# Four preactivated convolution layers, layer 3: a widest state for each query row, far key tiles scored at strips only and packed into banks, and two places a step for other products

## The chip, the cores and the metric

One core of one Trainium2 chip runs the whole kernel as one program. The metric is the device time of that program in microseconds, as the median of several runs. A profiled execution has a time of its own, which stands beside the others in the table below.

## The reference, cut to what matters

The input is an image batch `x` of 4 x 256 x 48 x 48 in float32. Each of four layers adds its own result to `x`, after a group norm `_gn`. Layers 0 to 2 are convolutions. Layer 3 is a box-window linear attention with 8 heads of 32 channels:

```python
q = sigmoid(einsum('bchw,oc->bohw', x, Wq)); k = sigmoid(einsum(..., Wk))
v = einsum(..., Wv); v = v / max(norm(v, axis=1), 1e-12)
Ik  = integral(k)
Ikv = integral(einsum('bfhw,bghw->bfghw', k, v))
for w in (1, 2, 4):                     # window of 48 / w rows and columns around each pixel
    wk, wkv = box(Ik, 48 // w), box(Ikv, 48 // w)
    attn = einsum('bdhw,bdfhw->bfhw', q, wkv)
    norm = einsum('bdhw,bdhw->bhw', q, wk)
    outs.append(attn / (norm[:, None] + 1e-06))
return einsum('bchw,oc->bohw', concatenate(outs, axis=1), Wout) + bout
```

For each pixel and each of three windows the result is the sum over the pixels in the window of (q . k) v, divided by the sum of (q . k). The windows reach 24, 12 and 6 pixels to one side, less one on the other (`HALVES`). There is no softmax, so a sum over keys that all queries of a set see may be taken as a state, the sum of k v^T, which q then multiplies.

## The kernel before, in words

Layers 0 to 2 take the span up to about 1412 us, layer 3 the rest. Near the end of layer 2 some of layer 3's projections are already made.

**Tiles of layer 3.** The 48 rows are six tile rows of `RB` = 8. A query block is one tile row of 8 x 48 = 384 queries (`NB`), of one image `b` and one half of the channels `ct` (four heads, `HG`). `order` runs over 4 images x 2 halves x 6 rows, 48 blocks. A key tile is 8 rows x 16 columns = 128 keys; a tile row `a` has three (`NKC`), index `c`. A block goes over all key tile rows that its widest window sees (`tiles_of`), at most three away, in two halves of the width (`PARTS`): that is one step, 60 for the six blocks of a half of the channels, 480 in all. Near tile rows (the smallest window sees them, at most one away) and far ones take turns.

**A step.** `Block.scores` multiplies keys by queries on TensorE into two PSUM tiles `s` of two banks each, two heads a tile, up to 512 columns a head; the four heads stand on four row strips of the array. A penalty product of bf16 (`picks`, `masks`) adds -1024 where the widest window does not see the key. `Block.masked` takes them out into `sm`: ACT (and, for tiles three rows away, DVE for one of the two pairs) applies a Relu for the widest window; DVE multiplies the middle window's part by a mask; POOL multiplies a part of that by the smallest window's mask. Two steps later (`LAG`) `Block.sums` multiplies `sm` by the values `vs` into three accumulators `acc0` to `acc2`, on four column strips of the array.

**The state.** For tile rows at most two away (`rows_whole`), a query column of the widest window sees whole key tiles except at strips (`strips`): 8 or 16 of the columns of a key tile. Only the strips are summed in steps; for the rest `state` makes k v^T of each tile row (keys transposed on TensorE, `keys_ps`; then `kv_ps`), `window_state` adds the rows that a query block sees on POOL into `kv`, and `Block.whole` multiplies it by the queries, one product for each head and key column, of 24 or 32 query columns by 8 rows (192 or 256 columns, three for each head). Tiles three rows away are in no state: they are scored and summed at all their columns, `rows_seen` giving 7 or 8 query rows.

**Other products.** Projections of the next image, key states, norms, output products and divisions are generators in `active`; `advance()` moves each by one `yield` and is called once a step, after the sums. The estimates `spare` (TensorE) and `slack` (POOL) say whether a job may go on in this step (`turn`, `bank`, `pool_turn`); all share the one PSUM bank `st` of `ps_m`. `until(...)` calls `advance()` until something is made, with no limit on cost. `FETCH` is the number of calls between a load's issue and its use. Every engine runs its instructions in the program's order, and SP issues nearly all loads and stores in one queue.

**Norms.** `k_sums` makes box sums of the keys (POOL, DVE's scans, ACT; stored to `kb_d` by way of `pt`); `norms` loads upper and lower rows (`nhi`, `nlo`) and the queries (`nq`), subtracts and multiplies on POOL, and sums on TensorE (`norm_ps`). `inverse`, `prepare` and `finish` divide, multiply by `Wout` (`out_ps`) and store. A block cannot begin before the block two before it is done, and that needs its norm.

All of layer 3's instructions carry line 244 in the profile, since a helper records them; they are told apart by the names of tiles.

Of the kernel before, what the change touches and what calls it, by code (L numbers as in the profile page):

```python
# [22 lines left out]
P = 128  # L23
# [4 lines left out]
RB = 8  # L28
# [56 lines left out]
MIDWAY, WHOLE = 3, 4  # L85
# [55 lines left out]


# [3 lines left out]
def penalties():  # L146

    got = []
    for half in range(2):
        got.append(((0, half), strips(half), None))  # L150
    for da, (r0, r1) in FAR_ROWS.items():
        for half in range(2):
            got.append(((da, half), PARTS[half], (r0, r1)))
    return got
# [22 lines left out]
def window_masks():  # L177
# [15 lines left out]
    for key, parts, rows in penalties():  # L193
        at = PENALTY_AT[key][0]
        for c, x0, x1 in parts:
            xs = np.arange(x0, x1)[None, :, None]
            ys = np.arange(*(rows or (0, RB)))[None, None, :]
            n = (x1 - x0) * ys.size
            kx = c * KC + np.arange(KC)[:, None, None]
            ky = key[0] * RB + np.arange(RB)[:, None, None]  # L200
            unseen = ~((xs - h <= kx) & (kx < xs + h)) & (ys == ys)
            costs[RB : RB + KC, at : at + n] = UNSEEN * unseen.reshape(KC, n)
            if rows is not None:
                unseen = ~((ys - h <= ky) & (ky < ys + h)) & (xs == xs)
                costs[0:RB, at : at + n] = UNSEEN * unseen.reshape(RB, n)
            at += n
    ms += [np.tile(m, (P // D, 1)) for m in (picks, costs)]
    return np.concatenate(ms + [column_taps()], axis=1).astype(np.float32)
# [39 lines left out]
def conv_preact_kernel(  # L248
# [75 lines left out]
    kf_d = [dram.tile([C, HW], F32, tag=f"kf{b}", name=f"kf_d{b}") for b in range(B)]  # L324
    kb_d = [dram.tile([NW, C, H, W], F32, tag=f"kb{b}", name=f"kb_d{b}") for b in range(B)]
# [14 lines left out]
    def advance(time=ALL, pool_time=ALL):  # L340
# [3 lines left out]
        spare = min(spare, 0.0) + time  # L344
        slack = min(slack, 0.0) + pool_time
# [57 lines left out]
    free = {"xr": 1, "xn": 2, "kt": 2, "sq": 2, "vt": 2, "cs": 1, "o": 2, "rc": 2, "res": 2}  # L403

    FETCH = 3
# [187 lines left out]
    with (  # L593
# [107 lines left out]
        def load_constants():  # L701
            sync.dma_start(out=w2_sb, in_=w2)
            sync.dma_start(out=b1_sb, in_=b1.rearrange("(p o) -> p o", o=1))
            sync.dma_start(out=taps, in_=masks_in[:QB, NMASK:])
# [918 lines left out]
    with (  # L1623
# [25 lines left out]
        nc.gpsimd.memset(zeros, 0.0)  # L1649
        head_sel = wts.tile([P, NCT, D], F32, name="head_sel")  # L1650
# [12 lines left out]
        inside = wts.tile([P, (RB + 1) * ROW], F32, name="inside")  # L1663
        nc.gpsimd.memset(inside, 1.0)
        for r in range(RB + 1):
            nc.gpsimd.memset(inside[:, r * ROW + GAP - 1 : r * ROW + GAP], 0.0)
# [10 lines left out]
        def k_sums(mo):  # L1677
# [14 lines left out]
            for at, (b, a) in enumerate(todo):  # L1692
# [27 lines left out]
                for i, j in ((0, n // 2), (n // 2, n)):  # L1720
                    dve.tensor_tensor_scan(
                        cs[:, i:j],
                        inside[:, i:j],
# [5 lines left out]
                    yield 1  # L1729
# [3 lines left out]
                pt = scr.tile([P, NW, RB, W], F32, tag="pt", name="pt")  # L1733
                for wi, h in enumerate(HALVES):
# [5 lines left out]
                    yield 1  # L1740
# [6 lines left out]
                )  # L1747
                made.add(("kb", b, mo, a))

        def norms(b, rb):  # L1750
# [4 lines left out]
            def load(ct):  # L1755
                chans = slice(ct * P, (ct + 1) * P)
                hi = scr.tile([P, NW, RB, W], F32, tag="nhi", name="nhi")
                lo = scr.tile([P, NW, RB, W], F32, tag="nlo", name="nlo")
                qf = scr.tile([P, NB], F32, tag="nq", name="nq")
                sync.dma_start(out=qf, in_=qr_d[b][chans, rb * NB : (rb + 1) * NB])  # L1760
                for wi, h in enumerate(HALVES):
# [7 lines left out]
                    if n < RB:  # L1769
# [3 lines left out]
                        )  # L1773

                    y0 = rb * RB - h - 1
# [5 lines left out]
                return hi, lo, qf  # L1781
# [5 lines left out]
            loaded = [load(ct) for ct in range(NCT)]  # L1787
            yield FETCH
            for hi, lo, qf in loaded:
# [9 lines left out]
                sums.append(hi)  # L1799
            yield 1  # L1800
# [49 lines left out]
        def state(b, ct, a):  # L1850
# [3 lines left out]
            yield FETCH  # L1854
            yield from bank(1, product_time(NKC * P))
# [15 lines left out]
            act.copy(states[b, ct][:, a], ps)  # L1871
            made.add(("state", b, ct, a))

        def window_state(i):
# [4 lines left out]
            yield from wait_for(*(("state", b, ct, a) for a in rows))  # L1879
            st = states[b, ct]  # L1880
            yield from pool_turn(NKC * D, len(rows) - 1, urgent=True)
            t = scr.tile([P, NKC, D], F32, tag="kv", name="kv", bufs=2)
            pool.tensor_add(t, st[:, rows[0]], st[:, rows[1]])
            for a in rows[2:]:
                pool.tensor_add(t, t, st[:, a])
            wides[i] = t
            made.add(("window", i))

        def load_q(b, ct, rb):
# [5 lines left out]
            return qs  # L1895
# [12 lines left out]

        class Block:


            def __init__(self, i, qs):
                self.i, self.qs = i, qs
                self.b, self.ct, self.rb = b, ct, rb = order[i]
                self.tiles = tiles_of(rb)
                self.todo = [
                    [(a, half) for a, half in self.tiles if seen(wi, a, rb)] for wi in range(NW)
                ]
                self.accs = self.stage = None

            def scores(self, a, half):
                r0, r1 = rows_seen(0, a, self.rb)
                ss = [ps_s.tile([P, 2, 512], F32, tag="s", name="s") for _ in range(NPR)]
                at = 0
                for c, x0, x1 in PARTS[half]:
                    n = (x1 - x0) * (r1 - r0)
                    for pr, s in enumerate(ss):
                        for j in range(2):
# [4 lines left out]
                                self.qs[head, x0:x1, r0:r1],  # L1933
                                start=(at == 0),
                                stop=False,
                            )
                    at += n
                lo, hi = strip_columns(half) if rows_whole(a, self.rb) else (0, at)
                first, n = PENALTY_AT[(0 if rows_whole(a, self.rb) else a - self.rb), half]
                for pr, s in enumerate(ss):  # L1940
                    for j in range(2):
                        g = 2 * pr + j
                        rows = slice(g * D, g * D + RB + KC)
                        pe.matmul(
                            s[:, j, lo:hi],
                            picks[rows, :],
                            masks[rows, PEN_AT + first : PEN_AT + first + n],
                            start=False,
                            stop=True,
                        )  # L1950
                return ss

            def parts(self, wi, a, half):

                if wi == 0:
                    return strips(half) if rows_whole(a, self.rb) else PARTS[half]
                return parts_seen(wi, half)

            def masked(self, a, half, ss):

                rb = self.rb
                r0, r1 = rows_seen(0, a, rb)
                wis = [wi for wi in range(NW) if seen(wi, a, rb)]
                full = rows_whole(a, rb)
                offset = {PARTS[half][0][0]: 0}
                offset[PARTS[half][1][0]] = (PARTS[half][0][2] - PARTS[half][0][1]) * (r1 - r0)
                left = {c: x0 for c, x0, _ in PARTS[half]}

                t = smp.tile([P, NPR * SM_ROOM], F32, tag="sm", name="sm")
                at, blocks_, views = 0, [], {}  # L1970
                for wi in wis:
                    y0, y1 = rows_seen(wi, a, rb)
                    ps = self.parts(wi, a, half)
                    for c, p0, p1 in ps:
                        if wi == 0:
                            continue
                        n = HG * (y1 - y0) * (p1 - p0)
                        views[wi, c] = t[:, at : at + n].rearrange(
                            "p (j x r) -> p j x r", j=HG, r=y1 - y0
                        )  # L1980
                        at += n
                    if wi > 0:
                        continue
                    n = sum(p1 - p0 for _, p0, p1 in ps) * (y1 - y0)
                    block = t[:, at : at + HG * n].rearrange("p (j n) -> p j n", j=HG)
                    blocks_ = [block[:, 2 * pr : 2 * pr + 2] for pr in range(NPR)]
                    at, o = at + HG * n, 0
                    for c, p0, p1 in ps:
                        m = (p1 - p0) * (y1 - y0)
                        views[wi, c] = block[:, :, o : o + m].rearrange(  # L1990
                            "p j (x r) -> p j x r", r=y1 - y0
                        )
                        o += m
                assert at <= NPR * SM_ROOM

                def times_mask(engine, wi, c, rows, cols, dst, src):
                    mr = rb * RB + rows[0] - (a * RB - HALVES[wi] + 1)
                    mc = cols[0] - (c * KC - MCOL0[wi])
                    nr, ncol = rows[1] - rows[0], cols[1] - cols[0]
# [5 lines left out]
                many = seen(NW - 1, a, rb)  # L2005

                def middle(s, pr):
                    y0, y1 = rows_seen(1, a, rb)
                    for c, p0, p1 in parts_seen(1, half):
                        at = offset[c] + (p0 - left[c]) * RB  # L2010
                        src = s[:, :, at : at + (p1 - p0) * RB].rearrange(
                            "p j (x r) -> p j x r", r=RB
                        )[:, :, :, y0:y1]
                        dst = views[1, c][:, 2 * pr : 2 * pr + 2]
                        times_mask(dve, 1, c, (y0, y1), (p0, p1), dst, src)

# [365 lines left out]
```

## Time and profile before

| | us |
|---|---|
| median of 3 runs | 3204.7 |
| lowest and highest run | 3195.62, 3205.02 |
| the profiled execution | 3220.09 |
| its span, first to last instruction | 3218.3 |
| first score product of layer 3, from the span's start | 1412.0 |

| busy in the span | us | share |
|---|---|---|
| TensorE matmul (PE) | 2886.4 | 90% |
| TensorE weight load (PEld, overlaps PE) | 2014.6 | 63% |
| VectorE (DVE) | 2004.0 | 62% |
| GpSimd (POOL) | 1351.2 | 42% |
| ScalarE (ACT) | 1018.9 | 32% |

The mean granted clock of TensorE is 0.952 of full speed. How to read the lines shown later: a group is a line, engine, operation, tiles written and read, shape and count, then busy us, mean ns of one, then the engine's idle time before them and what ended it. For TensorE, 32\*128 is the part of the array in use, rows by columns. An f32 matmul leaves two records. A timeline line is start, duration, engine, operation and count. A wait line is who waited for whom, us in total, times, and the longest.

### The profile page before, as it was taken

To read this page: it belongs to the slowest core of one execution; us is meant where nothing else is said; L and a number is where in the kernel's file an instruction comes from. 1 tells how busy PE (TensorE), PEld (TensorE's weight loads), DVE (VectorE), ACT (ScalarE), POOL (GpSimd) and SP (SyncE) were. 2 spreads that over 40 slices of the span, in tenths; PEclk is the share of its full clock that TensorE was granted. 3 is DMA by queue.
4 is the path that set the end of the run, shared out by engine and by line. 5 is a ranking of instruction groups with operands and counts; after the bars stand their busy time and mean duration, and the time that the engine had idled before them with its cause. 6 is when DMAs were issued, how large, how long until landed. Compare 5 with 4: busy or idle time off the path is not lost.

```text
span 3218.3 us, 97296 instructions
## 1 busy us (share of the span) xinstructions
PE 2886.4 (90%) x41802; PEld 2014.6 (63%) x41802; DVE 2004.0 (62%) x3907; ACT 1018.9 (32%) x2090; POOL 1351.2 (42%) x1916
## 2 busy tenths in 40 slices
PE   3678999899989978889996999998999999999999
PEld 2456768678776857576663665565566665666665
DVE  7976668647855731466774765676546775455454
ACT  0002211111111153326642335552336533333322
POOL 0000021003001221146788776877846777634443
PEclk9789899999999997989998999999999999999999
DMA  8746513431342253224466555554734455501222
GB/s 273 213 158 196 162 53 116 130 107 60 125 132 92 74 152 114 103 89 140 157 207 173 172 167 164 167 171 152 193 91 145 141 173 162 160 33 54 86 68 67
DMA packets 380033, 433.85 MB, mean 135 GB/s; under 512 B 129844, under 2 KB 335444, under 8 KB 378452
## 3 DMA queue, kind: packets, MB, share of 16 engines
q1 hardware_dynamic: 378403, 425.76, 42.9%
q8 instruction: 331, 5.42, 0.7%
q0 software_dynamic: 144, 1.08, 0.2%
q10 hardware_dynamic: 1056, 0.79, 0.1%
q14 instruction: 99, 0.80, 0.1%
HBM read 287.91 MB, written 140.68 MB: 133 GB/s over the span
## 4 chain that ended last, share of the span: by engine, by line
PE 60%; DVE 12%; POOL 4%; DMA 4%; ACT 4%; issue 3%; SPq 2%; ACTq 0%; DVEq 0%; POOLq 0%
PE s L244 16%; PE cv L244 15%; PE acc L244 14%; PE out_ps L244 5%; PE proj_ps L244 5%; DVE sm L244 3%; PE ap L244 2%; ACT sm L244 2%; SPq L244 2%; DVE l2v L244 2%; POOL nhi L244 1%; POOL sm L244 1%; DVE v L244 1%; PE keys_ps L244 1%; DVE x L244 1%
## 5 line engine op out<-in xcount | busy, mean ns | idle before, releaser
L244 DVE TENSOR_TENSOR sm<-s,masks 128x448 f32<-128x448 f32 (+11 forms) x1536 | 634.6, 470 | 465.5 <-PE s L244 431.5
L244 POOL TENSOR_TENSOR sm<-sm,masks 128x704 f32<-128x704 f32 (+11 forms) x512 | 595.2, 1184 | 559.1 <-DVE sm L244 558.7
L244 ACT ACTIVATE sm<-s 128x384 f32<-128x384 f32 (+2 forms) x864 | 467.5, 545 | 783.1 <-PE s L244 641.0
L244 PE MATMUL s<-qs,ks 32*128 32x320 f32 (+3 forms) x7680 | 601.6, 402 | 46.7 <-ACT sm L244 41.6
L244 PE MATMUL cv<-vx,wt 128*128 128x288 f32 x2080 | 561.6, 426 | 91.1 <-DVE vx L244 49.6
L244 PE MATMUL acc<-sm,vs 128*32 128x128 f32 (+20 forms) x17920 | 607.4, 279 | 1.4 <-issue 1.4
L244 PEld LDWEIGHTS s<-qs,ks 32*128 32x128 f32 x7680 | 376.9, 186 | 278.1 <-issue 111.0
L244 PEld LDWEIGHTS acc<-sm,vs 128*32 128x32 f32 x17920 | 430.2, 110 | 190.5 <-issue 137.6
L244 PEld LDWEIGHTS cv<-vx,wt 128*128 128x128 f32 x2080 | 403.4, 198 | 213.0 <-issue 54.1
L244 POOL MEMSET v<- 128x16 f32 (+1 forms) x120 | 18.7, 216 | 761.1 <-DVE vx L244 634.3
L244 PE MATMUL cv<-v,wl 128*128 128x384 f32 x1152 | 227.9, 358 | 25.1 <-issue 8.0
L244 PEld LDWEIGHTS cv<-v,wl 128*128 128x128 f32 x1152 | 217.7, 198 | 36.6 <-issue 16.4
L244 DVE TENSOR_SCALAR sm<-s 128x896 f32<-128x896 f32 (+1 forms) x96 | 110.9, 1155 | 144.4 <-PE s L244 125.4
L244 PE MATMUL s<-masks 24*128 24x192 bf16 (+2 forms) x1920 | 175.5, 268 | 0.0
L244 POOL TENSOR_TENSOR v<-l2v,v 128x384 fp32r<-128x384 f32 x96 | 108.5, 1160 | 119.3 <-ACT v L244 110.6
L244 PE MATMUL cv<-pad,wl 128*128 128x384 bf16 x864 | 145.5, 331 | 5.1 <-ACT pad L244 5.1
L244 POOL TENSOR_TENSOR nhi<-nhi,nq 128x384 f32<-128x384 f32 x144 | 147.8, 1048 | 0.0
L244 PEld LDWEIGHTS <-wl 128*128 128x128 bf16 x864 | 84.5, 98 | 65.6 <-issue 8.1
L244 PE MATMUL out_ps<-o,wout_sb 128*32 128x384 f32 x1152 | 119.8, 487 | 4.9 <-DVE res L244 2.2
L244 DVE TENSOR_TENSOR pt<-cs 128x184 f32<-128x184 f32 x144 | 119.8, 836 | 0.1
L244 PE MATMUL out_ps<-stage,wout_sb 128*32 128x384 f32 x1152 | 119.4, 486 | 0.0
L244 PE MATMUL ap<-seen,xT 120*128 120x120 f32 (+3 forms) x832 | 118.8, 302 | 0.0
(178 smaller groups left out, 3434.7 us busy)
## 6 DMA issues: line engine op xcount, KB each, us to landing
wt<-wt SPq DMA_DIRECT2D x48, 768.0 KB
kb_d<-pt SPq DMA_DIRECT2D x48, 576.0 KB
rc<-r_d SPq DMA_DIRECT2D x192, 144.0 KB
nhi<-kb_d SPq DMA_DIRECT2D x120, 192.0 KB
nlo<-kb_d SPq DMA_DIRECT2D x88, 192.0 KB
o_d<-stage SPq DMA_DIRECT2D x24, 576.0 KB
o<-o_d SPq DMA_DIRECT2D x24, 576.0 KB
wl<-wl_d SPq DMA_DIRECT2D x16, 768.0 KB
```

The source lines that it names most:

```text
L244: return lambda *args, **kwargs: self.tc.keep_in_program_order(op(*args, **kwargs))
```

## The change

- Tile rows two or three away get one step for their strips of all three key columns (384 columns, or 336 where 7 rows are seen) instead of two steps of 512 or 448. The middle window's pieces of tile rows two away are scored apart, each put into the first far step whose bank has room; where none has, a step without strips is added. Tile rows at most one away stay as they were. A half of the channels has 50 steps instead of 60.
- So that tiles three away need strips alone, the state now depends on the query's row: `window_state` makes `wide`, eight states, one for each query row. Seven of them hold a part of the far tile row's keys: the values are multiplied by 0 or 1 per key (`row_parts`, 21 ACT copies), multiplied by the transposed keys (`part_ps`, 12 products of 224 columns), and added to the base on DVE. The transposed keys are stored by `state` to `kt_d` and loaded again. `Block.whole` makes a product for each key column, query row and head, of 24 or 32 columns; it reads the queries in another order, `qr`, which is loaded beside `qs`.
- All widest Relus are on ACT.
- `advance()` is called twice a step: before the sums with the step's estimate, and after them with none. The whole state is added at step 2 of a block and not 4 (`WHOLE`); `window_state` of the next block starts when a block begins and not midway; `FETCH` is 5 calls and not 3. In the first pass the key tile rows are loaded one block earlier.
- `norms` loads the lower rows and the queries of one half of the channels at a time, from single buffers, the second after the first half's POOL work. `pt` has one buffer. DVE's two scans are cut at a row.

```diff
-MIDWAY, WHOLE = 3, 4
+MIDWAY, WHOLE = 3, 2
...
-    FETCH = 3
+    FETCH = 5
...
+        if time is not None:
+            spare = min(spare, 0.0) + time
+            slack = min(slack, 0.0) + pool_time
...
+            lo, qf = load_lower(0)
             yield FETCH
-            for hi, lo, qf in loaded:
+            for ct, hi in enumerate(loaded):
...
+                if ct + 1 < NCT:
+                    lo, qf = load_lower(ct + 1)
+                    yield FETCH
...
             act.copy(states[b, ct][:, a], ps)
+            sync.dma_start(out=kt_d[b][ct, a], in_=kt.rearrange("p c n -> p (c n)"))
...
+            keys = scr.tile([P, NKC, P], F32, tag="keys1", name="keys1", bufs=1)
+            sync.dma_start(out=keys.rearrange("p c n -> p (c n)"), in_=kt_d[b][ct, far])
+            yield from pool_turn(NKC * D, len(rows), urgent=True)
+            base = scr.tile([P, NKC, D], F32, tag="kv", name="kv", bufs=2)
+            wide = scr.tile([P, NKC, RB, D], F32, tag="wide", name="wide", bufs=2)
...
+            if above:
+                pool.tensor_copy(wide[:, :, 0], base)
+            else:
+                pool.tensor_add(wide[:, :, 0], base, st[:, far])
...
+                part = scr.tile([P, HG, RB - 1, D], F32, tag="part", name="part", bufs=1)
+                for y in range(RB - 1):
+                    at = y if above else RB - 1 + y
+                    act.activation(
+                        part[:, :, y], vs, AF.Identity, scale=row_parts[:, at : at + 1]
+                    )
+                    if y % 3 == 2:
+                        yield 1
...
+                    pe.matmul(
+                        ps[head, at : at + n],
+                        keys[:, c, head],
+                        part[:, g].rearrange("p y d -> p (y d)"),
...
+                dve.tensor_add(
+                    wide[:, c0 : c + 1, 1:],
...
+            for n, a, c in sorted(middles, key=lambda m: -m[0]):
+                fits = [st for st in far if st.columns + n <= 512]
+                if not fits:
+                    far.append(Step(rb))
...
-                if full:
-                    widest(act, *second)
-                    middle(*first)
-                    widest(act, *first)
-                    middle(*second)
-                else:
-                    widest(act, *first)
-                    widest(dve, *second)
+                widest(*second)
+                middle(*first)
+                widest(*first)
+                middle(*second)
...
-                            t[head, c, :],
-                            self.qs[head, c0:c1],
...
+                                self.accs[0][head].rearrange("p (w r) -> p w r", w=W)[:, c0:c1, y],
+                                t[head, c, y, :],
+                                self.qr[head, y, c0:c1],
...
+            advance(max(time, 500.0), max(pool_time, 150.0))
             if n >= LAG:
...
-            advance(max(time, 500.0), max(pool_time, 150.0))
+            advance(None)
```

## The prediction, made before the changed kernel ran

> **What bounds the kernel now.** I read the page's busy times first, then the windows of layer 3, then its groups by shape, then TensorE's timeline, then the waits. A measurement of this kernel can tell about 0.3%, 10 us, from no change.
>
> ```profile
> span 3218.3 us, 97296 instructions
> ...
> PE 2886.4 (90%) x41802; PEld 2014.6 (63%) x41802; DVE 2004.0 (62%) x3907; ACT 1018.9 (32%) x2090; POOL 1351.2 (42%) x1916
> ```
>
> ```profile
> core 0: us, PE busy (x) PEld busy (x) DVE busy (x) ACT busy (x) POOL busy (x), PEclk, DMA share, GB/s
> 1412.00:3218.00 1806.00, 1701.67 (x35968) 1075.11 (x35968) 1088.85 (x2138) 739.05 (x1566) 1174.27 (x1510) 0.98 0.46 138
> ```
>
> The first score product starts at 1412 us, so layer 3 has 1806 us; all the rest is outside the change. In them TensorE is 94% busy, POOL 65%, DVE 60%, ACT 41%, at a granted clock of 0.98. A busy PE is not a PE at its peak, so the instructions themselves come next (the groups by shape; then two steps of TensorE's timeline).
>
> ```profile
> L244 ACT ACTIVATE sm<-s 128x384 f32<-128x384 f32 x768 | 374.3, 492 | 645.9 <-PE s L244 508.9 <-DVE sm L244 123.0 <-POOL sm L244 3.5
> ...
> L244 DVE TENSOR_SCALAR sm<-s 128x1024 f32<-128x1024 f32 x48 | 58.6, 1222 | 67.1 <-PE s L244 57.2 <-POOL sm L244 6.4 <-POOL nhi L244 3.4
> ...
> L244 ACT ACTIVATE sm<-s 128x1024 f32<-128x1024 f32 x48 | 49.2, 1025 | 69.2 <-PE s L244 68.6 <-POOL nhi L244 0.6
> ...
> L244 ACT ACTIVATE xn<-xr,st 128x384 f32<-128x384 f32 x60 | 42.1, 707 | 10.8 <-DMA xr<-x_d 10.8
> ...
> L244 PE MATMUL kv_ps<-vs,keys 128*32 128x32 f32 x1152 | 18.6, 197 | 2.5 <-ACT keys L244 2.5
> ...
> L244 ACT COPY state<-kv_ps 128x96 f32<-128x96 f32 x48 | 11.4, 238 | 11.2 <-PE kv_ps L244 10.8
> ```
>
> ```profile
> 2506.29 1.15 PE L244 MATMUL s<-qs,ks 32*128 32x320 f32 x16
> 2507.26 0.26 PE L244 MATMUL s<-masks 24*128 24x192 bf16 x4
> 2507.45 1.53 PE L244 MATMUL acc<-sm,vs 128*32 128x160 f32 x48
> 2508.80 1.05 PE L244 MATMUL proj_ps<-wv_sb,xn 128*32 128x256 f32 x16
> 2509.78 1.15 PE L244 MATMUL s<-qs,ks 32*128 32x320 f32 x16
> ```
>
> One step: scores, penalties, sums of the step two before, one other product; then the next step. An f32 product leaves two records, and four heads run side by side on strips of the array. From the records' start times, a record of n columns follows the one before, for all four heads together, after n/1.2 + 2.5 ns: 268 ns at 320, 109 at 128, 56 at 64 columns, and 31 at kv_ps's 32. So an f32 product costs 1.67 ns a column, a bf16 one 0.42. Added up over layer 3 this gives 1419 us. Of the 383 us that remain, some 168 are fixed per step: 110 ns from the penalties to the sums, 112 from there to the next scores, 105 for the scores' second weights, 24 in the sums, 0.35 us x 480 steps. The rest waits: the evacuation of the score bank (about 76 us by the sum below), stalls over 0.8 us (83 us; one of 15.6 us is in the first line below), and small change. So TensorE's own stream is the bound, and what shortens it shortens the kernel.
>
> ```profile
> PE norm_ps L244 <- POOL nhi L244: 26.2, 5, 15.6
> ...
> POOL nhi L244 <- DMA nlo<-kb_d: 24.7, 5, 11.8
> ```
>
> **The change part by part** (counts from the two built programs; eight passes, one for each image and channel half).
>
> *Scores.* Per pass the score columns of one head fall from 30336 (60 steps) to 24248 (50 steps): far tiles are scored at 384 or 336 strip columns, and their middle pieces fill the rest of the bank. 6088 x 8 x 1.667 ns = -81 us.
>
> *Widest sums.* Only the three-tiles-away rows shrink, from 5760 to 2160 columns a pass: -3600 x 8 x 1.667 ns = -48, with the halves of the middle pieces joined -49 us.
>
> *Penalties*, bf16: 14976 to 11376 columns a pass: -12 us.
>
> *Whole state by row.* Three four-head products of 192 or 256 columns, two records each (1.08 us), become 24 of 24 or 32 columns, 48 records. The nearest row is kv_ps: 31 ns for four heads. 48 x 31 = 1.49 us, x 48 query rows: +20 us. Bounds: 28 ns (the fastest kv_ps) +13; 56 ns (64 columns) +78. kv_ps has the same columns, so 31. The Trainium skill speaks against this part ("TensorEngine Tiling (Array Packing)", Instruction Overhead: each matmul has some 60 cycles of overhead, so a very short moving side saves nothing). If each record paid that alone, 192 x 25 ns = 4.8 us a row would be an estimate of +179 us instead of +20 and the forecast would turn to slower; the kv_ps records, four of them in 31 ns, show the four strips sharing it.
>
> *Part products.* 144 four-head products of 224 columns, 378 ns each: +54.5 us, same strip form as the sums, so no new switch.
>
> *Fewer steps.* 480 to 400: 80 x 0.35 = -28 us.
>
> TensorE's stream: -81 - 49 - 12 + 20 + 54.5 - 28 = **-96 us**. One projection group moves from layer 2's end into layer 3, 5 us off one and on the other: 0.
>
> *Evacuation.* The trace has the last score read 2.11 us after the scores' end in near steps, 1.42 and 1.66 at two and three tiles' distance. A far step now has two Relus of 768 elements: 492 + 384 x 0.833 = 812 ns each (slope: (1025 - 492)/640), with 0.2 us of start 1.85 us. I set each against the products that the program has between the scores of that step and the next. Before, 178 steps wait 0.43 us, 76 us; after, 116 wait 0.43 us, 50 us, because a step holds more sums and up to two other products: **-26 us**. What is late next there is the one product bank, which a step now wants twice.
>
> *ACT.* Relus: -256 x 0.492 - 48 x (1.025 + 0.918) + 176 x 0.812 + 48 x 0.732 = -41 us. The 1008 row-scaled copies of 128 elements, each with a scale from a tile: below, state's copy of 96 elements without one, 238 + 27 = 265 ns; above, xn with scale and bias, 707 - 256 x 0.833 = 494. I take the middle, 380 ns: +383 us. ACT becomes 1081 us, 62% of the layer. Cover: the time in which TensorE does sums and other products, 2 us or more a step; a run of three copies is 1.1 us and stands before the next Relus. The Trainium skill ("ScalarE: Activation LUTs", What ACT_TABLE_LOAD costs) gives 186 ns + 93 for a pointer operand + 0.833 ns per element, an estimate of 386 ns, so it too speaks against many short activations; by it the sum is the same, and no run yet shows this form.
>
> *DVE.* The 96 Relus go (58.6 above and 52.3 for the 896 form: -111), joined middles -19, wide's adds at 620 and 390 ns (the sm products of 448 and 224) +48: -82 us. DVE idles 40%, so this counts only through the evacuation, where far steps now end on ACT instead.
>
> *POOL.* +24 copies and +24 adds of 0.4 us: +18, to 1192 us; hidden except where norms are late. window_state starts at its block's begin and not midway, so its adds (4 x 0.41 us) and its load on SP go ahead of half a block of norms, key sums and stores; they were urgent before: 0.
>
> *DMA.* 144 more of 192 KB, 28 MB on about 250: share 0.46 to 0.53. SP's queue is in order: a second lower load of the norms, keys' store and load and qr now stand in it, and with one buffer the norms' load waits for POOL, and v, q and kp transfers behind it. POOL waits for that load, the n2 masks behind POOL.
>
> *What is new on the path.* The first block must have the far tile's state, and the whole at step 2, not 4: one chain of keys, state and 21 copies at the start, +6 (0 to 13). The norms' second load shows where the order has them forced together with the output products (steps 84, 100 and 200): 3 x 5 us, the mean of the 24.7 us wait, +15 (0 to 60). ACT runs ahead of Relus, one product bank for two places a step, pt with one buffer: 0.06 us a step, +25 (-10 to 90, by 0.22 us a step, a fifth of a run of copies). **+46 us.**
>
> Sum: -96 - 26 + 46 = **-76 us**. The profiled execution, 3220.1 us (span 3218.3 and 1.8 around it), would be 3144; the median of the runs, 3204.7, lies 15 below it: **3129 us**.
>
> **The rivals.**
> *ACT in the way (slower).* 432 runs of copies stand in ACT's queue; where one starts late (part has one buffer, so it waits for TensorE's product), the Relus behind it are late, and with them the scores. For: 9 runs per query row on 8 steps, and evacuation is already within 0.5 us of the next scores in half the steps. Against: ACT is idle 38%. It decides from 122/400 = 0.3 us a step; at 0.45 us, under half a run, +58: 3263. Chance 0.14.
> *POOL holds the pace.* From 1600 to 1850 us POOL is busy 203 of 250 us. If it sets the first three passes (750 of 1806 us), 42% of the 122 us gained is lost there, and the norms' loads cost 30: -122 + 51 + 30 + 6 = -35: 3170. Against: POOL idles over 3 us at a time waiting for DVE there. Chance 0.20.
> *Short products at 56 ns.* +58 on the forecast: -18, 3187. Chance 0.06.
> *Covers hold.* The +46 falls away: -122, 3083. Chance 0.12.
> *Not as described* (row products not ready and forced): the built order has them ready in most blocks; left in the +46.
>
> **How the numbers follow.** Forecast 0.48, between -45 and -110. Faster: 0.48 + 0.20 + 0.12 and two thirds of the short products, 0.84 less 0.02 for POOL's tail = 0.82; within 0.3% 0.04; slower 0.14. The range runs from 3070, beyond "covers hold" by the 13 us of its lower bounds, to 3225, past the short products and the near part of the slow rival; beyond lie about 0.07 and 0.11.
>
> **What would show it.** After: no TENSOR_SCALAR on sm; s at 0.81 us Relus; 48 whole groups of about 1.5 us; part copies near 0.38 us; layer 3 near 1730 us with 400 steps of 4.3 us. Wrong: whole groups near 2.7 us; PE waiting for ACT sm over 100 us in total (42 now, in 92 waits); norm waits over 60 us; steps above 4.5 us.

## The result and the profile after

The changed kernel took 3523.7 us (median of 4 runs, 3522.7 to 3524.6), the kernel before 3204.9 us on the same chip (median of 4, 3195.6 to 3207.0): a ratio of 1.100 [1.098, 1.102], 319 us slower. The forecast was 3129 us, the range ended at 3225. The profiled execution took 3524.55 us (before 3220.09).

The page's head and layer 3 as one window (the same columns as in the prediction):

```profile
span 3522.7 us, 113922 instructions
...
PE 2928.0 (83%) x49850; PEld 2082.2 (59%) x49850; DVE 1937.8 (55%) x3779; ACT 1257.3 (36%) x2967; POOL 1367.2 (39%) x1960
```

```profile
1412.00:3522.00 2110.00, 1745.39 (x43986) 1141.67 (x43980) 1017.59 (x1994) 979.59 (x2448) 1187.66 (x1555) 0.91 0.44 132
```

The window begins 9 us behind the first score product, which now starts at 1402.8 us. In it layer 3 took 2110 us instead of 1806. TensorE's share of it fell from 94% to 83%, its granted clock from 0.98 to 0.91, and no other engine is near its limit (POOL 56%, DVE 48%, ACT 46%). The time is in TensorE's gaps, not in a new bound. The groups by shape, in that window:

```profile
L255 ACT ACTIVATE part<-vs,row_parts 128x128 f32<-128x128 f32 x1008 | 329.7, 395 | 85.6 <-PE part_ps L255 80.3 <-issue 5.3
...
L255 ACT ACTIVATE sm<-s 128x768 f32<-128x768 f32 x176 | 133.7, 809 | 94.3 <-PE s L255 86.2 <-DVE sm L255 3.2 <-POOL kv L255 2.5
...
L255 PE MATMUL part_ps<-part,keys 128*32 128x224 f32 x1152 | 91.5, 391 | 89.0 <-ACT part L255 39.0 <-DMA keys<-kt_d 36.7 <-DVE res L255 4.7
...
L255 PE MATMUL acc<-qr,wide 32*32 32x24 f32 x6144 | 83.2, 193 | 74.6 <-issue 74.5
```

The prices of single instructions were right: the copies 395 ns (380 forecast), the far Relus 809 (812). What the forecast did not have is in the last column: 89 us of idle TensorE before the part products, and 75 us before the short whole products of 24 columns that ended for nothing the profile names ("issue"; 16 more before those of 32). One step of the timeline shows where that is:

```profile
1585.41 0.86 PE L255 MATMUL keys_ps<-ident,ks 128*32 128x128 f32 x24
1586.20 1.16 PE L255 MATMUL acc<-qr,wide 32*32 32x24 f32 x115
1588.77 0.85 PE L255 MATMUL acc<-qr,wide 32*32 32x32 f32 x77 [1.41 <-issue]
1589.55 1.06 PE L255 MATMUL acc<-sm,vs 128*32 128x117 f32 x32
```

A whole group is 192 records. Here 115 ran, TensorE then had nothing for 1.41 us, and the other 77 followed. The best groups took 1.62 us (1.49 forecast), the median group 3.87 us, the longest 9.07, all with the same records. The waits of layer 3:

```profile
PE acc L255 <- issue: 106.0, 53, 4.9
...
PE part_ps L255 <- ACT part L255: 39.0, 33, 3.5
PE part_ps L255 <- DMA keys<-kt_d: 36.7, 8, 8.5
...
PE proj_ps L255 <- ACT sq L255: 36.2, 13, 12.2
...
PE s L255 <- ACT sm L255: 23.3, 33, 3.7
```

Two of them in the kernel before:

```profile
PE s L244 <- ACT sm L244: 41.6, 92, 2.7
...
PE acc L244 <- issue: 1.4, 3, 0.7
```

TensorE's wait for the evacuation of the score bank fell from 41.6 us to 23.3. That it is the packing's gain is not shown: in the runs below it lies anywhere from 11.5 (e9) to 55.1 us (e12), and at 54.5 in e3, which has the same packing. The wait in the accumulators, 1.4 us before, became 106.

**What the stall inside a group is.** One line of the page's DMA queues, of the kernel before and of the changed one:

```profile
q8 instruction: 331, 5.42, 0.7%
```

```profile
q8 instruction: 392, 6.42, 0.8%
```

This queue's packets are 16384 bytes each. TensorE's records (matmuls and weight loads) are 2 x 41802 before and 2 x 49850 after; with the 1208 and 835 semaphore and drain instructions that the trace has beside them, 256.2 and 256.5 a packet, 64 bytes each. So the queue brings TensorE's own instructions, some 256 a packet. I then counted, in the trace's records, how many of all these TensorE had run whenever a stall over 0.8 us inside a whole group ended, 42 of them in this kernel. In all 42 that number was 256 times the packets landed so far plus 193 or 194, and the packet had landed 1.20 to 1.60 us before. The same remainder each time means that TensorE stopped at the same place of a block, and went on once the next had landed: it had run everything that had arrived. In layer 3 a packet started with a median of 217 records still in hand, took 1.04 us to land, and where TensorE stalled its first record ran 2.43 us (median) after the packet's start. A whole group of 384 records (192 and their weight loads) at 1.49 us uses 217 in 0.84 us. I call these stalls, wherever they fall, *delivery*: the gap before the first record of a block, ended within 1.8 us of its landing.

The Trainium skill ("Runtime: NRT & Kernel Launch", Instruction fetch mechanics) says that instructions are refilled in blocks of 16 KiB, 256 of them, which this count confirms, and that crossing a block is mostly hidden. Here it was not hidden: 66 such stalls, 131.5 us, where the kernel before has 5 of 4.7 us in all.

**Layer 3 taken apart.** *Stream* is the prediction's sum over TensorE's records; *clock* is the extra time of records that ran at half clock; *other* is what is left: the fixed steps between kinds of products, and waits for other engines and transfers. All are us of one profiled execution of each kernel, from its first score product to TensorE's last record. The stream counts a short whole product at the forecast's 31 ns a record; at the median such a record follows after 33 ns.

| kernel | layer 3 | stream | delivery | clock | other |
|---|---|---|---|---|---|
| before | 1802 | 1419 | 5 | 21 | 357 |
| after | 2115 | 1356 | 132 | 122 | 506 |
| whole as before, row 0 (e1) | 1936 | 1337 | 3 | 74 | 522 |
| neither whole nor parts (e3) | 1864 | 1282 | 5 | 74 | 503 |
| e3, one place (e5) | 1723 | 1277 | 10 | 37 | 399 |
| e3, waits doubled (e7) | 1756 | 1290 | 1 | 38 | 427 |
| change, whole spread (e8) | 2001 | 1356 | 57 | 80 | 507 |
| before + short whole (e11) | 1977 | 1439 | 128 | 57 | 354 |
| before + two places (e12) | 1889 | 1424 | 11 | 34 | 420 |

Against before, the changed kernel's stream fell by 63 us, as the prediction's column terms say (-81 - 49 - 12 + 20 + 54.5 = -67.5). It lost 127 us to delivery, 101 to the clock, 149 to other waits.

### The profile page after: what moved, and what is told of

Read it like the earlier page. It is cut to its first block, busy times and chain, and to the rows that moved or that the text cites. A ratio compares the mean times of both kernels' runs of the same rounds, so it can differ in the third digit from the quotient of the medians.

```text
span 3522.7 us, 113922 instructions
## 1 busy us (share of the span) xinstructions
PE 2928.0 (83%) x49850; PEld 2082.2 (59%) x49850; DVE 1937.8 (55%) x3779; ACT 1257.3 (36%) x2967; POOL 1367.2 (39%) x1960
## 5 line engine op out<-in xcount | busy, mean ns | idle before, releaser
L255 DVE TENSOR_TENSOR sm<-s,masks 128x448 f32<-128x448 f32 (+9 forms) x1408 | 628.6, 498 | 881.6 <-PE s L255 764.2
L255 ACT ACTIVATE sm<-s 128x384 f32<-128x384 f32 (+2 forms) x736 | 415.2, 582 | 755.7 <-PE s L255 609.5
L255 PE MATMUL acc<-sm,vs 128*32 128x128 f32 (+16 forms) x16512 | 581.3, 284 | 16.3 <-issue 15.3
L255 PE MATMUL s<-qs,ks 32*128 32x128 f32 (+6 forms) x8320 | 521.2, 361 | 41.2 <-ACT sm L255 26.5
L255 PEld LDWEIGHTS acc<-sm,vs 128*32 128x32 f32 x16512 | 457.4, 114 | 148.7 <-issue 97.7
L255 ACT ACTIVATE part<-vs,row_parts 128x128 f32<-128x128 f32 x1008 | 329.7, 395 | 85.6 <-PE part_ps L255 80.3
L255 PE MATMUL acc<-qr,wide 32*32 32x24 f32 (+1 forms) x9216 | 104.2, 195 | 90.9 <-issue 90.7
L255 PE MATMUL part_ps<-part,keys 128*32 128x224 f32 x1152 | 91.5, 391 | 89.0 <-ACT part L255 39.0
L255 PEld LDWEIGHTS acc<-qr,wide 32*32 32x32 f32 x9216 | 93.9, 111 | 109.9 <-issue 107.1
L255 PE MATMUL s<-masks 24*128 24x192 bf16 (+2 forms) x1472 | 130.8, 278 | 1.8 <-issue 1.8
```

The costliest lines, as they stand in the source:

```text
L255: return lambda *args, **kwargs: self.tc.keep_in_program_order(op(*args, **kwargs))
```

## The experiments

All ratios are to the kernel before, run on the same chip, with the 95% interval.

**First set: which part costs.** Run e1 puts the whole state back to three four-head products, e2 leaves the row parts out, e3 does both, and e4 has the full change with one place a step.

```diff
 # e1 (and e3), in Block.whole
-    for y in range(RB): ... t[head, c, y, :], self.qr[head, y, c0:c1]
+    t[head, c, 0, :], self.qs[head, c0:c1]
 # e2 (and e3), in window_state
-    keys ... part ... pe.matmul(ps[...], keys, part) ... dve.tensor_add(wide[:, c0 : c + 1, 1:], ...)
 # e4
-    FETCH = 5          # and yields of 2 in k_sums
+    FETCH = 3          # and yields of 1
-    advance(max(time, 500.0), max(pool_time, 150.0))    # ahead of the sums
-    advance(None)                                       # behind them
+    advance(max(time, 500.0), max(pool_time, 150.0))    # behind them
```

> The whole state goes back to three four-head products of 192 or 256 columns, made with row 0 of the new state for all eight query rows (rows 1 to 7 of the state are still made, and left out of the sum); all else stays. Theory A, TensorE outruns the delivery of its instructions in the 192 short records of a query row, and the stalls let the clock fall: 112 us of stalls inside the groups, 20 us of stream, and a third of the 101 us lost to the clock go, 3524 - 165 = about 3360 us (3330 to 3400), stalls inside the whole group near 3 us in total. Theory B, the row products and the two places share one bank and their chain stops TensorE: only the stream's 20 us go, about 3500 us.

Measured: 3336.5 us, 1.040 [1.038, 1.043]: 187 us less than the change. The short products are the largest single cost. From e1 to the change, stream is +19, delivery +129 and clock +48; the other waits do not grow.

> The row parts are left out: no ACT copies, no part products, no adds into the eight states, no store and load of the transposed keys; the 24 short products per query row stay and all read row 0 of the state. Theory A: the 54 us of products and some clock go, 3524 - 75 = about 3450 us, stalls in the whole groups as before (100 us and more). Theory B: the 54 us go, and with them most of the 190 us that TensorE waits before products for ACT part, ACT sq, the keys' load and the wide adds, and half of the clock's loss: about 3260 us (3220 to 3310).

Measured: 3452.1 us, 1.076 [1.073, 1.079]: 72 us less. Between e1 and e3 the same part is worth 81 us. Their four-head products were priced at 54.5, so the parts cost 17 to 27 us more than their stream: noticeable, not the cause.

> Both at once: no row parts, and the whole state in three wide products with row 0. What is left of the change is the packing of the far tiles, the Relus on ACT and two places a step. A alone: 3360 - 75 = 3285. B alone: 3260 - 20 = 3240. Both causes, adding up: 3524 - 165 - 265 = about 3095, which is what the forecast's TensorE stream gives for packing alone (3205 - 96 - 75 + 25 = 3060) with some waits. If it stays above 3200, the packing or the two places cost by themselves.

Measured: 3255.5 us, 1.014 [1.010, 1.018]. With both costs gone and 137 us less stream the kernel is still slower than before, so there is a third cause, in the other waits (503 against 357) and the clock (74 against 21).

```profile
ACT carry L255 <- POOL kp L255: 111.5, 35, 12.6
...
PE proj_ps L255 <- ACT sq L255: 51.0, 17, 12.3
```

These are e3's waits of layer 3. ACT stood 111.5 us at `carry`, a copy in the box sums of the keys, for POOL's sum before it (27.4 us before). ACT runs in order, so the copies, squares and Relus behind it stood too, and TensorE for those.

> Other products have one place a step again, after the sums, and the waits counted in places are those of before (a fetch of 3, 1 after each scan and difference); all else as changed. Theory A: no change, 3500 to 3550 us. Theory B with the two places at fault (a second product waits for the bank that the first holds): 100 us and more faster, 3400 or less. If it is slower, two places are needed to get the row products done in time: 3600 and more.

Measured: 3642.2 us, 1.135 [1.131, 1.139], 118 us more than the change. With the parts in it a block's `window_state` has nine more turns, for which one place a step may be too few; that was not tried by itself. At any rate neither setting of the places suits the full change.

**Second set: the third cause.** Theory P: the places. A generator's wait is counted in calls of `advance`; with two calls a step the same `yield 1` is half as long, so products and ACT's copies are put into the program before POOL or a load is done. Theory Q: SP's queue, the norms' second load waiting for POOL with all loads behind it. e5 is e3 with one place; e6 is e3 with the norms' loads as before, two buffers each; e7 is e3 with two places and each wait counted double.

```diff
 # e6
-    nlo, nq, pt: bufs=1, load_lower(ct + 1) behind the first half's work
+    nlo, nq, pt: two buffers, loaded with nhi        # room from wide: one row, qr: one buffer
 # e7
-    entry[0] = step + wait
+    entry[0] = step + 2 * wait                       # FETCH 3, yields of 1
```

> The kernel without row parts and with three wide whole products (row 0 for all rows), now with one place a step after the sums and the waits counted as before (fetch 3, 1 after each scan and difference). It took 3255 us with two places. Theory P, two places make each job's waits half as long in time, so ACT and TensorE stand before results that are not there (ACT carry waits 111 us for POOL kp, 27 before): 3255 - 100 or more, 3090 to 3160. Theory Q, SP's queue is held by the norms' single-buffered lower load (it waits 129 us for POOL nhi, 2 before) and late stores hold ACT: little change, 3220 to 3270. Theory R, packing itself or fewer steps are at fault (jobs no longer done in time): slower, 3280 and more, as one place was with the row parts (3642 against 3524).

> The same kernel without row parts and short products, two places kept, but every wait of a job counts double (a fetch 6 places, after a yield of 1 two places), so each job moves as often as with one place a step while the jobs spread over both places. Theory P: the waits of ACT carry for POOL and of TensorE for ACT sq fall to before's, about 3150. Theory Q: 3240 to 3260. Theory R: slower than 3280.

Measured: e5 3142.9 us, 0.979 [0.976, 0.983], e7 3139.0 us, 0.979 [0.976, 0.983]. Both take some 115 us off e3, as P said; like e3 they are without the row parts' work. Not all of it falls in layer 3 for e7, whose doubled waits act on the projections near the end of layer 2 too: its first score product starts at 1366 us, against 1403 in e3. In e5 it starts at 1414 us, so e5's whole gain is layer 3's. By the table's profiled executions layer 3 takes 108 us less in e7 than in e3, and 141 less in e5. Of the kernels run that do all of the work, none came under the kernel before. What e7 still shares with e3 is the second place; what it changes is the length of the waits. In e7 the wait at `carry` is

```profile
ACT carry L255 <- POOL kp L255: 49.1, 16, 8.8
...
PE acc L255 <- POOL wide L255: 30.0, 6, 16.3
```

less than half of e3's, though not the 27.4 of before. The second line is new: TensorE waits for POOL's base state, which now is needed at step 2.

> The same kernel without row parts and short products, two places kept, but the norms load both halves' lower rows and queries at once from two buffers, as before, and pt has two buffers (the eight states' tile is cut to the one row that is read, to make room). Theory Q: SP's wait for POOL nhi falls from 129 us to under 10, ACT's waits for the stores of v, q and pt from 89 us to under 20, and the time to 3255 - 90 = about 3165. Theory P: 3230 to 3260, with ACT carry still waiting 100 us for POOL.

Measured: 3251.2 us, 1.015 [1.011, 1.018], as e3 (3255.5). SP's wait for POOL's `nhi` fell from

```profile
SPq L255 <- POOL nhi L255: 128.6, 23, 11.2
```

in e3 to

```profile
SPq L255 <- POOL nhi L255: 2.2, 4, 1.1
```

in e6, and the time did not move. The reverse shows it too: in e7, the fastest of these kernels, that wait is longer than in e3.

```profile
SPq L255 <- POOL nhi L255: 148.7, 21, 17.6
```

Theory Q falls.

**Third set: the short products and mends.** e8 is the change with the whole products of one key column in each of steps 2, 3 and 4. e9 is e8 with the waits doubled except in `window_state`.

```diff
 # e8
-    if at == WHOLE: blocks[i].whole(i)
+    if WHOLE <= at < WHOLE + NKC: blocks[i].whole(i, at - WHOLE)
 # e9
-    entry[0] = step + wait
+    entry[0] = step + entry[2] * wait                # entry[2]: 2, for window_state 1
```

> The changed kernel in full, but the 24 short four-head products of a query row are made in three parts, one key column in each of three steps, so that 64 short records stand between long ones and not 192 in a row. Theory A (TensorE's instructions are not delivered fast enough): the 98 us of stalls over 0.8 us inside the groups fall to under 30, the switches add 48 x 2 x 0.22 = 21 us, the clock gives back 20 to 40: 3524 - 100 = about 3425 us. If only the number of instructions counts and not where they stand: 3520 to 3545.

Measured: 3402.4 us, 1.062 [1.058, 1.066], 121 us less than the change with the same records in the same shapes. Delivery fell from 132 to 57 us, the clock's part from 122 to 80 (117 together), the other waits stayed (506, 507). TensorE's wait in the accumulators:

```profile
PE acc L255 <- issue: 26.9, 31, 4.4
```

So it is not the short product as such that is dear, nor its strided reads and writes, which e8 keeps, but 384 records in a row. Spreading does not win all of it back: e8 is 66 us over e1, and has 57 us of delivery where e1 has 3.

> The changed kernel in full with both remedies: the short products of a query row in three parts over three steps (3402 us by itself), and every job's waits doubled except those of the row parts (fetch 3, so 6 places; 1 after a scan, so 2). If the two add up as they did apart (116 us from the waits without the parts): 3402 - 100 = about 3300 us (3270 to 3340), still above before's 3205, since the parts' 54 us and the waits round them (72 to 81 us in all) stay. If the doubled waits bring more forced finishes (the built order has 16 places with over 4 us of other products, 8 before this edit): 3380 to 3450.

Measured: 3380.8 us, 1.054 [1.051, 1.057]: 22 us less than e8, where e7 had won 116. And these 22 us are not layer 3's: e9's first score product starts at 1367 us, e8's at 1411, and layer 3 takes 2012 us in e9 and 2001 in e8. The built order had 16 places with over 4 us of other products, against 8 in e8; that the longer waits win nothing here because of such forced finishes was not tried by itself. In TensorE's waits the parts stand high:

```profile
PE part_ps L255 <- ACT part L255: 70.8, 46, 9.7
```

**Fourth set: each part alone on the kernel before.** e11 adds only the short whole products, e12 only the two places, e10 only the packing of tiles two rows away (three away are scored whole, as before; 464 steps).

```diff
 # e11, in Block.whole of the kernel before
-    t[head, c, :], self.qs[head, c0:c1]                      # 192 or 256 columns
+    for y in range(RB): t[head, c, :], self.qr[head, y, c0:c1]   # 24 or 32
 # e12
+    advance(max(time, 500.0), max(pool_time, 150.0))         # ahead of the sums
-    advance(max(time, 500.0), max(pool_time, 150.0))         # behind them
+    advance(None)
-    FETCH = 3
+    FETCH = 5                                                # yields of 2 in k_sums
 # e10
+    steps_of(rb) with add_strips for |a - rb| == 2, add_far for 3
```

> The kernel before with only the short whole products: the same state used by all rows, but in 24 four-head products of 24 or 32 columns per query row, with the queries in row order (192 KB more to load per block). Theory A: +20 us of stream, some 100 us of stalls inside the groups, and 20 to 50 us by the clock: 3205 + 150 = about 3355 us (3320 to 3380). By the forecast's price alone: 3225.

Measured: 3390.0 us, 1.057 [1.054, 1.059], 184 us more than before. In the table stream is +20, which is the forecast's own price by the way it is counted, delivery +123 and clock +36, 179 together, while the rest stays (354, 357). Three lines of the waits and the timeline:

```profile
PE acc L244 <- issue: 105.2, 60, 5.0
```

```profile
2304.06 1.42 PE L244 MATMUL acc<-qr,kv 32*32 32x24 f32 x146
2307.45 0.59 PE L244 MATMUL acc<-qr,kv 32*32 32x24 f32 x46 [1.97 <-issue]
...
2405.09 1.81 PE L244 MATMUL acc<-qr,kv 32*32 32x24 f32 x192
```

The last line is a group that met no empty block: 192 records in 1.81 us, to the end of the last one (1.62 to its start, as the best groups above). The first two are one that ran dry after 146.

> The kernel before with only the two places a step: a first call before the sums with the estimate, a second after them with none, a fetch of 5 and waits of 2 after scans and differences as in the change. Theory P (the waits, counted in places, become half as long in time): 3205 + 60 to 120, about 3290, with ACT carry waiting over 80 us for POOL kp (27 before). If the two places by themselves harm nothing: 3190 to 3215.

Measured: 3293.9 us, 1.027 [1.024, 1.030], 88 us more than before, as much as P gave. By the table its layer 3 is 87 us longer, 63 of them in *other*. It has no row state and no packing:

```profile
ACT carry L244 <- POOL kp L244: 83.8, 32, 6.2
```

In the kernel before that line is

```profile
ACT carry L244 <- POOL kp L244: 27.4, 12, 6.0
```

> The kernel before with the packing alone, for tiles two away, whose state needs no rows: one step of strips, middle pieces packed into banks; tiles three away scored at all their columns in two steps, one Relu on DVE; whole state in three wide products; one place a step, fetch 3, both norms' loads at once. 464 steps. TensorE's stream: -33 us of scores, -6 us of switches: 3205 - 39 = 3166 if the waits stay; 3160 to 3215, since the steps that go were the ones in which other products stood. A version that would beat both.

Measured: 3233.6 us, 1.007 [1.005, 1.010]: a miss. The stream fell by 33 us, to 1386, but other waits rose from 357 to 404. The wait at `s` for ACT is 51.6 us with one of 11.1; before it was 41.6, the longest 2.7. Fewer steps also mean fewer places for other products; that this is the reason was not tried.

## Why the prediction was wrong

By the runs, from one kernel to the next: before 3205; the change without row parts, short products and the second place (e5) 3143, -62; with two places a step (e3) 3255, +113; the row parts' work (e1) 3336, +81; the short whole products (after) 3524, +187.

**The step that failed most: "48 x 31 = 1.49 us, x 48 query rows: +20 us".** The cadence was nearly right: at the median a record followed after 33 ns, and the best group ran in 1.62 us. The term measured 184 us by e11 and 187 by e1. I took the price from `kv_ps`, whose groups are 24 records long; such a row shows how fast TensorE runs records that it has, not how fast they come. The bounds, 13 to 78 us, were both cadences and so had the same hole. The rival of 56 ns a product had the right place and the wrong mechanism. The rule about overhead that I weighed, at +179, comes near the total by chance: e8 keeps every product and is 121 us faster, and the best group ran in 1.62 us and not 4.8, which a cost per product can't give.

**"One product bank for two places a step ... 0.06 us a step, +25."** e12 measured +88 and e3 against e5 +113, at and over the upper bound of 90. I priced the bank and ACT's order and did not ask what a second call of `advance` does to waits that are counted in calls. `FETCH` rises from 3 to 5 calls, 2.5 steps instead of 3, and most `yield 1` stay.

**Not priced at all: the clock.** The sum has no term for it; I carried 0.98 over as a constant. Time at half clock in layer 3 went from 85 to 370 us, and cost 101 us more.

**The part products, +54.5 of stream,** measured 72 (e2) and 81 (e1 to e3). The waits for `part` and for the keys' load (39.0 and 36.7 us) were in "ACT in the way" and "POOL holds the pace", but hit the part products and not the scores.

**Evacuation, -26, and fewer steps, -28.** The forecast's sum had 76 us of this wait in the kernel before, the wait line has 41.6; it fell by 18, but not by the packing alone, as said above. The steps' share can't be told apart in the other waits. e5 has 142 us less stream, and its layer 3 is only 79 us shorter: 42 come back in *other*, 16 as clock, 5 as delivery. Which waits, beyond the lines shown, is open.

**The norms' second load, +15,** did not show as TensorE's wait in the changed kernel: `norm_ps` waited 3.4 us for POOL's `nhi`, against 26.2 before.

**The slow rival, ACT in the way of the Relus,** is not what happened: PE waiting for `sm` was to be over 100 us and is 23. **POOL holds the pace** by the norms' load: e6 and e7 refute the load's share. Of the signs that I named, two came: "whole groups near 2.7 us", at 3.87, and "steps above 4.5 us", at 5.3 (2115 us, 400 steps). Right were the built order (400 steps), the column counts and every instruction price that had a row of its own kind.

## What to carry to other kernels

Before many long products are cut into short ones, count records as well as columns: a run of several hundred TensorE records at 30 ns for four strips uses up what has been delivered, whatever the cadence row says, and spreading them over steps gives much of it back. Where a schedule counts its waits in calls, another call per step changes every wait; lengthen them with it, or test the places by themselves first (lengthening won 108 us of layer 3 in e7, and nothing there in e9, which does all of the work). And a term that opens idle time on TensorE should carry a second one for the clock.

## What the runs showed of the hardware

- *Delivery of instructions.* TensorE's records come in packets of 256 on a queue of their own. The shortest time seen between two landings in layer 3, over all the kernels run, was 3.14 us (82 records a us), while a whole group at 1.49 us asks for 258 a us. e11's 35 stalls inside whole groups end at the same count as the changed kernel's 42, all of them, 0.89 to 1.74 us behind a landing. In about half of the changed kernel's 66 delivery stalls the packet had started late, with 40 records or fewer in hand instead of some 217; why is open.
- *Clock.* Half-clock stretches last 3.41 us or a multiple of it (6.83, 10.24): 10 of them in layer 3 before, 53 after. The Trainium skill ("TensorE: Matmul & The Clock Gate", Part 1) gives an idle window of about 3.4 us as the trigger of half speed. The lengths agree with that window, but here it need not be idle: 52 stretches begin within the changed kernel's layer 3, whole multiples of 3.41 us apart, and in the 3.41 us before each TensorE's matmuls and weight loads took 0 to 60% of the time (median 39%; only 6 were idle throughout). Windows of that grid after which the clock stayed full had 47% or more. Stalls over 0.8 us were 361 us in the changed kernel's layer 3 and 83 before; the 278 us more came with 101 us of slower records.
